# A graph network layer on one core: two small products of a node block move ahead of the node product, and VectorE's share of column copies begins four steps later

## The chip, the core and the metric

The kernel runs on one core of one Trainium2 chip. The metric is the device time of one execution in microseconds (us); a lower time is better. Five engines take part, each with its own instruction stream in a fixed order: TensorE (PE, with its weight loads shown as PEld), VectorE (DVE), ScalarE (ACT), GpSimd (POOL) and SyncE (SP). They wait for each other through semaphores.

## The reference

There are 12,500 nodes with 64 features and 200,000 edges, sorted by their target node. For each edge the reference takes the features of its source and its target, runs them through a two-layer network, does the same with the edge's own 64 features, multiplies the two results and a cutoff factor that depends on the edge's distance, and adds the product to the target node. The sums then go through one more two-layer network per node, and the result is normalised.

```python
nodes = node_state[edges].reshape(num_edges, -1)
gates = ssp(edge_state @ We1 + be1) @ We2 + be2
soft_cutoff = 1.0 - jax.nn.sigmoid(5.0 * (edges_distance - (CUTOFF - 1.5)))
h = ssp(nodes @ Wn1 + bn1) @ Wn2 + bn2
messages = h * (gates * soft_cutoff)
message_sum = jnp.zeros_like(node_state).at[edges[:, 1]].add(messages)
new_state = node_state + (ssp(message_sum @ Ws1 + bs1) @ Ws2 + bs2)
x = _layernorm(x + new_state)          # ssp(v) = softplus(v) - log 2
```

## The kernel before

**Steps.** The edges are cut into 391 steps of 512, each of four lanes of 128 edges (`K = 4`). One loop (variable `i`, from -1) runs all of them in a software pipeline that is written out by hand: the order in which the source issues instructions is the order on each engine. In iteration `i` the first layer of step `i + 1` and the second layer of step `i` are worked on.

**One iteration on TensorE**, in this order: the two biases (`layer1_bias` L299, `layer2_bias` L342); the scatter product of step `i - 2` (`scatter`, L371), whose result is added to the running sums; four transposes of the gathered source features of step `i + 1` (`transposes`, L286, into a tile named tx, of which there are two buffers); the edge product (`layer1_edge`, L304); in most iterations from 91 on the *unread product* (`busy_before_node`, L337), which multiplies constants into a place of the tile z that the next product overwrites and that nothing reads before; the node product (`layer1_node`, L311), which has to wait for ScalarE's copy xT of the transposes; and the second layer (`layer2`, L349 and L354). Up to iteration 90 a table of node products is still being made, one piece for each iteration (`chunk`, L641), in the place where the unread product stands later.

**ScalarE** copies the transposes (xT, L294), makes its column copies, and then the exponential and the logarithm for step `i + 1` (L325, L328). **VectorE** adds the scatter product of the iteration to the sums (`window`, L391), forms the message (`hcut` L363, `message` L367), the softplus of step `i + 1` (L333), the one-hot matrix of step `i + 3` (L280) and its own column copies. The exponential (L325) and `window` read the same tile z, and `window` comes after the exponential.

**Gathers.** POOL fetches the source features of a lane with one indirect DMA (L204), four for each step. The tile xg that they land in has eight buffers, so POOL runs ahead: while TensorE is in iteration `i`, the gathers of step `i + 6` are waiting for the buffer of step `i - 2`, that is for the scatter product of iteration `i`.

**Columns.** For some lanes there is no gather. The features of all nodes also lie transposed in SBUF (xh), and an engine copies the 128 columns of such a lane one by one (L262), 16 in each iteration: ScalarE for lane 2, VectorE for lane 1. Such a lane takes eight iterations, after which VectorE picks the valid half of each column (`choose`, two instructions L274 for each half, so two for each lane), and the node product gets a second part (L314). Which steps have such a lane is worked out by `slots_by_columns`: ScalarE's are taken first, and VectorE's must not be next to one of them. With `COLUMNS_FROM = 8` for both engines, ScalarE's steps are 18, 26, 34, ..., VectorE's 20, 28, 36, ..., 47 of each, and both engines finish a lane in the same iteration (15, 23, 31, ...). The function `four` tells whether a step has four gathers; where step `i + 5` has only three, the unread product of iteration `i` is left out.

**Node blocks.** The nodes are cut into 25 blocks. When the sums of a block are complete, its last network runs in ten parts that are spread over the following iterations by `BLOCK_STEPS`: two of them have TensorE products (`hidden`, L410, which reads the sums; and `layer2` of the block, L438 and L441, which reads a tile that VectorE makes in `ssp`, L433), the others run on ScalarE, VectorE and SP. `hidden` stands two iterations after the block is complete, the block's `layer2` six. In the iteration where one of the two products is due, it is issued after `layer2(i)` of the edges, and its counterpart on VectorE after the softplus. 24 of the blocks have both products inside the loop; the last one comes behind it.

Of the kernel before, what the change touches and what calls it, by code (L numbers as in the profile page):

```python
# [25 lines left out]
P = 128  # L26
# [8 lines left out]
AHEAD = 3  # L35
# [5 lines left out]
BEHIND = 5  # L41
# [3 lines left out]
BLOCK_STEPS = ((2, 3, 4, 4, 6, 7, 8, 9, 10, 14), (2, 3, 3, 4, 5, 6, 7, 8, 9, 10), (1, 2, 1, 2, 3))  # L45
COLUMNS = (16, 16)
BASES = 4
COLUMNS_FROM = 8
XH_PARTS = 4
CUTOFF = 5.0  # L50
EPS = 1e-5
# [4 lines left out]
def node_blocks(N):  # L56

    first = N % NB
    assert N > NB and first % 2 == 0 and first <= HE
    sizes = ([first] if first else []) + [NB] * (N // NB)  # L60
    return [(sum(sizes[:i]), n) for i, n in enumerate(sizes)]


def block_steps(N, NG):

    steps = []
    for at, n in node_blocks(N):
        share = sqrt(min(1.0, (at + n) / N))
        spread = sqrt(share * (1.0 - share) / (NG * GE))
        steps.append(ceil(NG * (share + SPREADS * spread)))  # L70
    return steps


def slots_by_columns(NG):

    slots, taken = [], set()
    for queue in (1, 0):
        columns, n = COLUMNS[queue], 0
        for g in range(NG - 2):
            if (g - 3 - COLUMNS_FROM + 1) * columns >= (n + 1) * P and not {g - 1, g, g + 1} & taken:  # L80
                slots.append((queue, g, queue + 1))
                taken.add(g)
                n += 1
    return sorted(slots)
# [20 lines left out]
def gnn_resnorm_kernel(ctx: ExitStack, tc: tile.TileContext, a: dict, out: bass.AP, E: int):  # L105
# [30 lines left out]
    def tx_tile():  # L136
        return psum.tile([P, NB], F32, name="tx")
# [54 lines left out]
    def padding(g, k):  # L192
        return g * GE + k % 2 * HE + k // 2 * P >= E
# [15 lines left out]
    def four(g):  # L209
        return g < NG and not any(padding(g, k) or (g, k) in by_columns for k in range(K))  # L210
# [21 lines left out]
    own = [[slot for slot in slots if slot[0] == queue] for queue in range(2)]  # L232
    column_tiles, side_tiles, chosen_columns = {}, {}, {}
    column_at, columns_done, whole = [[], []], [0, 0], []

    def columns_left(i, queue):
        return len(own[queue]) * P - columns_done[queue] if i >= COLUMNS_FROM else 0

    def read_columns(i, queue):

# [38 lines left out]
    def onehot(g):  # L279
        last = nc.vector.tensor_tensor(xgs[g][:, :, D:DW], iota, rel[:, g, :].to_broadcast([P, K, W]), OP.is_equal)  # L280
        note(("onehot", g), last)
# [75 lines left out]
    def layer2(g):  # L357
        layer2_edge(g)
        layer2_node(g)
# [121 lines left out]
    with tc.manual_schedule():  # L481
# [64 lines left out]
        def lowest(first, last):  # L546
            part = low[:, first:last]
            nc.vector.tensor_reduce(part, dst_h[:, first:last], AX.X, OP.min)
            nc.vector.tensor_scalar(part, part, 0.0, None, OP.max)
            nc.vector.tensor_tensor(part, part, most[:, first:last], OP.min)  # L550
            n = last - first
            nc.vector.tensor_tensor(spread[:, first:last],
                                    ident.rearrange("p (r q) -> p r q", r=1).to_broadcast([P, n, P]),
                                    part.to_broadcast([P, n, P]), OP.mult)
# [22 lines left out]
        for i, w in enumerate((we2[:D, 0, :], wn2)):  # L577
            n = w.shape[0]
# [83 lines left out]
        with tc.tile_pool(name="finish", bufs=1) as finish:  # L662
            blocks = list(zip(node_blocks(N), block_steps(N, NG)))
            last = NG - 1
            parts, begun, complete, rest = {}, None, 0, []

            def at(f, g, *more):
                if 0 <= g < NG:
                    f(g, *more)

            def behind_by(i):
                close = last - CLOSE
                return [g for g in ([i - 2] if i <= close else []) + ([i - 1] if i >= close else []) if g >= 0]

            for g in range(LOADS - 1):
                load(g)
            for g in range(2):
                onehot(g)
            lowest(1, NR)
            everywhere(1, NR)  # L680
            clear(0, CHUNKS)
            highest()
            for i in range(-1, last - 1):
                now = parts.pop(i, [])
                early = [part for part in now if part.tensor]
                at(load, i + LOADS)
                if i >= 0:
                    at(gather, i + AHEAD, range(K), [("transposes", i)] if i < BEHIND else ())
                layer1_bias(i + 1)
                at(layer2_bias, i)  # L690
                for n, g in enumerate(behind_by(i)):
                    scatter(g, zs[i + 1][:, 1, HE + 2 * n * W : HE + 2 * (n + 1) * W])
                transposes(i + 1, ("load", i + 1), ("gather", i + 1), ("onehot", i + 1))
                xcopy(i + 1)
                columns(i, 1, finish)
                layer1_edge(i + 1)
                c = chunk_of(i, NCH)
                if c is None and four(i + AHEAD + BEHIND - 3):
                    busy_before_node(i + 1)
                if c is not None:  # L700
                    beside_sums = zs[i + 1][:, 1, HE + 2 * W : HE + 2 * W + P]
                    chunk(c, beside_sums)
                layer1_node(i + 1)
                exps(i + 1)
                logs(i + 1)
                if c is not None:
                    keep_chunk(c, beside_sums)
                read_columns(i + 1, 1)
                for g in behind_by(i):
                    window(g)  # L710
                if c is not None:
                    clear(c, c + 1)
                at(layer2, i)
                for part in early:
                    part.tensor(tx_tile())
                at(hcut, i)
                at(message, i)
                softplus(i + 1)
                for part in early:
                    part.others()  # L720
                at(onehot, i + 3)
                read_columns(i, 0)
                columns(i, 0, finish)
                choose(finish)
                for part in now:
                    if not part.tensor:
                        part.others()
                for action in beside.get(i, []):
                    action()
                complete = i  # L730
                if blocks and complete >= blocks[0][1] - PREPARE and not begun:
                    begun = node_block(*blocks[0][0], finish)
                    begun.pop(0).others()
                if blocks and complete >= blocks[0][1]:
                    steps = next(steps for steps in BLOCK_STEPS if i + steps[-1] < last - 1)
                    for n, part in zip(steps, begun):
                        parts.setdefault(i + n, []).append(part)
                    rest = begun[len(steps) :]
                    blocks.pop(0)
                    begun = None  # L740
            assert len(blocks) == 1 and begun and not parts


            begun.pop(2).others()
            transposes(last, ("load", last), ("gather", last), ("onehot", last))
            xcopy(last)
            layer1_bias(last)
            layer2_bias(last - 1)
            scatter(last - 2, zs[last][:, 1, HE : HE + 2 * W])
            layer1_edge(last)  # L750
            layer1_node(last)
            for some in (edge, node):
                exps(last, some)
                logs(last, some)
            square, variance, root, scale, store = (part.others for part in rest)
            square()
            window(last - 2)
            for g in range(last - 1, last + 1):
                if g not in window_at:
                    window_bases(g)  # L760
            layer2(last - 1)
            layer2_bias(last)
            softplus(last, edge)
            layer2_edge(last)
            softplus(last, node)
            layer2_node(last)
            hcut(last - 1)
            message(last - 1)
            scatter(last - 1, tx_tile()[:, : 2 * W])
            variance()  # L770
            root()
            hcut(last)
            message(last)
            scatter(last, tx_tile()[:, : 2 * W])
            window(last - 1)
            window(last)
            hidden, clamp = begun.pop(0)
            hidden(gh_tile())
            scale()
            clamp()  # L780
            store()
            for part in begun:
                node_part(part)
# [5 lines left out]
    with tc.If(far > 0), tc.tile_pool(name="outside", bufs=1) as o:  # L789
# [7 lines left out]
        with tc.For_i(0, NG, 1) as g:  # L797
# [51 lines left out]
            for b in range(NBL):  # L849
# [5 lines left out]
                part = sums[:D, b * NB : (b + 1) * NB]  # L855
# [90 lines left out]
```

## Time and profile before

| what | value |
|---|---|
| median of 3 runs | 2354.7 us (2352.55 to 2364.48) |
| the profiled execution's own time | 2351.35 us |
| its span in the profile | 2349.3 us |
| mean granted TensorE clock | 0.964 |
| busy: PE, DVE, ACT, POOL | 85%, 65%, 64%, 59% of the span |

The profile is of one execution. In its rows, a line such as "L311 PE MATMUL z<-xT,wns" means the instruction of source line 311 on TensorE that writes the tile z from xT and wns; "x4" is a count, since a product of 32-bit numbers is shown as two matmuls for each one in the source; a name in square brackets is the idle time of the engine just before, and what ended it. PEclk is the granted share of the TensorE clock. A view by windows gives, for each stretch from A to B in us, its length and then the busy time of the engines with their number of instructions, the clock, the share of the DMA engines and GB/s.

### The profile page before, as it was taken

The numbers are of one execution on the slowest core, as the hardware profiler recorded it, in microseconds if no ns is written. First come the engines' busy times: TensorE is split into PE (matmuls) and PEld (weight loads), VectorE is DVE, ScalarE is ACT, GpSimd is POOL, SyncE is SP. The second block draws the span as 40 slices with busy tenths as digits, with TensorE's granted clock in tenths as the row PEclk, the third lists the DMA queues.
The fourth block names the chain that finished last, engine by engine and source line by source line (L and its number), as shares of the span: only waits on it lengthen the run. The fifth ranks groups of instructions, "written<-read, shape, count | busy, mean of one in ns | idle before, by whom it ended". The sixth has DMA issues, their size and how long they took to land.

```text
span 2349.3 us, 49245 instructions
## 1 busy us (share of the span) xinstructions
PE 1986.8 (85%) x12011; PEld 1549.9 (66%) x12011; DVE 1536.7 (65%) x9110; ACT 1511.8 (64%) x7412; POOL 1391.5 (59%) x1473
## 2 busy tenths in 40 slices
PE   6788888888888888888888888888888888888877
PEld 4676666666666666666666666666666666666665
DVE  4467666666666666666666667666666676667655
ACT  3466667666666666666667667666666666666653
POOL 6556666566666566666656566665666665556550
PEclk8799999999999999999999999999999999999988
DMA  6332232322222222222222222222222222222220
GB/s 190 95 83 71 64 70 57 79 62 74 60 59 57 54 62 54 59 56 61 55 58 63 52 61 63 59 59 58 59 59 59 59 61 60 55 56 59 60 51 13
DMA packets 162385, 149.51 MB, mean 64 GB/s; under 512 B 40564, under 2 KB 112021, under 8 KB 161962
## 3 DMA queue, kind: packets, MB, share of 16 engines
q1 hardware_dynamic: 114650, 96.55, 15.1%
q0 software_dynamic: 47008, 48.23, 10.9%
q8 instruction: 101, 1.65, 0.3%
q14 instruction: 192, 1.57, 0.2%
q10 hardware_dynamic: 434, 1.50, 0.2%
HBM read 136.50 MB, written 9.62 MB: 62 GB/s over the span
## 4 chain that ended last, share of the span: by engine, by line
PE 76%; issue 12%; DVE 6%; ACT 2%; DVEq 2%; another core or an unknown queue 1%; DMA 1%; POOL 0%; ACTq 0%; POOLq 0%
PE z L311 17%; PE gh L354 13%; PE z L371 10%; PE tx L286 9%; PE gh L349 8%; PE z L304 6%; PE z L337 4%; PE gh L342 3%; PE z L299 3%; DVE column L262 2%; DVEq L245 2%; ACT xT L294 1%; PE tx L410 1%; PE z L314 1%
## 5 line engine op out<-in xcount | busy, mean ns | idle before, releaser
L204 POOL DMA_INDIRECT xg<-in_x,src_i x1469 | 1391.3, 947 | 905.6 <-PE tx L286 378.3
L294 ACT COPY xT<-tx 106x512 f32<-106x512 f32 x391 | 228.6, 585 | 736.1 <-PE tx L286 704.6
L311 PE MATMUL z<-xT,wns 106*128 106x256 f32 x1564 | 464.1, 416 | 270.5 <-issue 238.0
L262 ACT COPY column<-xh 128x4 uint8 x6016 | 608.8, 193 | 0.0
L311 PEld LDWEIGHTS z<-xT,wns 106*128 106x128 f32 x1564 | 273.8, 197 | 420.4 <-issue 336.4
L262 DVE COPY column<-xh 128x4 uint8 x6016 | 486.4, 199 | 11.9 <-issue 6.9
L363 DVE TENSOR_TENSOR h<-gh,cut 128x256 f32<-128x256 f32 x391 | 166.0, 425 | 380.3 <-PE tx L286 260.8
L354 PE MATMUL gh<-consts,s 128*128 128x64 f32 x3128 | 400.2, 272 | 0.0
L354 PEld LDWEIGHTS gh<-consts,s 128*128 128x128 f32 x3128 | 389.6, 196 | 0.1
L328 ACT ACTIVATE u<-u,one 128x768 f32<-128x768 f32 x392 | 365.8, 933 | 13.5 <-ACT u L325 0.8
L333 DVE SCALAR_TENSOR_TENSOR s<-u,z 128x768 f32<-128x768 f32 x392 | 369.3, 942 | 0.4 <-issue 0.3
L391 DVE TENSOR_TENSOR sums<-sums,z 64x42 f32 x778 | 149.4, 192 | 325.5 <-issue 243.1
L325 ACT ACTIVATE u<-z 128x768 f32<-128x768 f32 x392 | 314.7, 803 | 47.2 <-PE z L311 25.5
L371 PEld LDWEIGHTS z<-xg,msg 128*128 128x128 f32 x1556 | 208.9, 195 | 140.9 <-issue 123.4
L371 PE MATMUL z<-xg,msg 128*128 128x84 f32 x1556 | 269.9, 297 | 13.6 <-DVE msg L367 13.5
L349 PEld LDWEIGHTS gh<-consts,s 128*128 128x128 f32 x1564 | 218.8, 196 | 92.7 <-DVE s L333 68.3
L349 PE MATMUL gh<-consts,s 128*128 128x128 f32 x1564 | 269.8, 296 | 11.8 <-issue 7.2
L286 PE MATMUL tx<-consts,xg 128*106 128x128 f32 x1564 | 243.9, 280 | 0.0
L304 PE MATMUL z<-eT,consts 128*128 128x256 f32 x782 | 243.7, 395 | 0.0
L286 PEld LDWEIGHTS tx<-consts,xg 128*106 128x106 f32 x1564 | 187.1, 145 | 1.2 <-issue 1.2
L367 DVE TENSOR_TENSOR msg<-gh,h 128x256 f32<-128x256 f32 x391 | 165.9, 424 | 13.4
L342 PE MATMUL gh<-row,ones 3*128 3x512 bf16 x391 | 149.3, 382 | 0.0
(107 smaller groups left out, 1193.4 us busy)
## 6 DMA issues: line engine op xcount, KB each, us to landing
eT<-in_eT SPq DMA_DIRECT2D x195, 256.0 KB
xg<-in_x,src_i POOLq DMA_INDIRECT x1469
wns<-table SPq DMA_DIRECT2D x782, 21.0 KB
table<-tb SPq DMA_DIRECT2D x14, 448.0 KB
side<-in_sides SPq DMA_DIRECT2D x94, 64.0 KB
y<-in_x SPq DMA_DIRECT2D x24, 128.0 KB
out<-y SPq DMA_DIRECT2D x24, 128.0 KB
xh<-in_xh SPq DMA_DIRECT2D x2, 781.5 KB
```

What stands on the lines that cost most here:

```text
L204: behind(note(("gather", g), nc.gpsimd.indirect_dma_start(out=xg[:, k, :D], out_offset=None, in_=x, in_offset=bass.IndirectOffsetOnAxis(ap ...
L262: copy(column_tiles[slot].bitcast(U8)[:, 4 * r : 4 * r + 4], xh[:, bass.ds(column_at[queue][j] - xh_at, 4)])
L286: ins = nc.tensor.transpose(tx[:, k, :], xgs[g][:, k, :DW], ident)
L294: note(("xcopy", g), nc.scalar.copy(xT, xTs[g]))
L304: nc.tensor.matmul(zs[g][:, 0, :HE], we1.rearrange("a h d -> a (h d)"), eTs[g], start=False, stop=True, skip_group_check=True)
L311: nc.tensor.matmul(zn, wns[:, g % REST, h, :], xTs[g][:, h], start=True, stop=not chosen, skip_group_check=True)
L325: nc.scalar.activation(us[g][:, part], z_of(g)[:, part], AF.Exp)
L328: nc.scalar.activation(us[g][:, part], us[g][:, part], AF.Ln, bias=one)
L333: nc.vector.scalar_tensor_tensor(ss[g].rearrange("p i t e -> p (i t e)")[:, part], us[g][:, part], BIG, z_of(g)[:, part], OP.min, OP.max)
L349: nc.tensor.matmul(v[:, 0, t], ss[g][:, 0, t, :], we2, start=False, stop=False, skip_group_check=True)
L354: nc.tensor.matmul(ghs[g][:, 1, 2 * t + h, :], ss[g][:, 1 + h, t, :], wn2, start=False, stop=h == 1 and t == 1, skip_group_check=True)
L371: ins = nc.tensor.matmul(sc, msgs[g][:, 2 * t : 2 * t + 2, :].rearrange("p h f -> p (h f)"), xgs[g][:, 2 * t : 2 * t + 2, D:DW], start=t = ...
```

## The change

It has two parts. The two TensorE products of a node block (`hidden` and the block's `layer2`) are issued in front of the node product of the same iteration instead of behind the second layer, and in those iterations the unread product is left out. Their counterparts on the other engines stay where they were. And `COLUMNS_FROM` becomes a pair, 12 for VectorE and 8 for ScalarE: VectorE's column copies begin in iteration 12, so its lanes are those of steps 22, 30, 38, ..., in the middle between ScalarE's 18, 26, 34, ...; it has 46 of them instead of 47, and finishes them in iterations 19, 27, 35, ....

```diff
-COLUMNS_FROM = 8
+COLUMNS_FROM = (12, 8)
...
-            if (g - 3 - COLUMNS_FROM + 1) * columns >= (n + 1) * P and not {g - 1, g, g + 1} & taken:
+            if (g - 3 - COLUMNS_FROM[queue] + 1) * columns >= (n + 1) * P and not {g - 1, g, g + 1} & taken:
...
     def columns_left(i, queue):
-        return len(own[queue]) * P - columns_done[queue] if i >= COLUMNS_FROM else 0
+        return len(own[queue]) * P - columns_done[queue] if i >= COLUMNS_FROM[queue] else 0
...
                 c = chunk_of(i, NCH)
-                if c is None and four(i + AHEAD + BEHIND - 3):
+                for part in early:
+                    part.tensor(tx_tile())
+                if c is None and not early and four(i + AHEAD + BEHIND - 3):
                     busy_before_node(i + 1)
...
                 at(layer2, i)
-                for part in early:
-                    part.tensor(tx_tile())
                 at(hcut, i)
                 at(message, i)
```

TensorE, in an iteration with a block's first product (L410, `hidden`; L311 is the node product, L354 the end of the edges' second layer). Before:

```order
L304 MATMUL z<-eT,consts 128x256
L311 MATMUL z<-xT,wns 128x256 x2
L349 MATMUL gh<-consts,s 128x128 x2
L354 MATMUL gh<-consts,s 128x64 x4
L410 MATMUL tx<-sums,consts 128x256 x2
L299 LDWEIGHTS be_82
L299 MATMUL z<-ones_81,be_82 128x256
```

and with the change:

```order
L304 MATMUL z<-eT,consts 128x256
L410 MATMUL tx<-sums,consts 128x256 x2
L311 MATMUL z<-xT,wns 128x256 x2
L349 MATMUL gh<-consts,s 128x128 x2
L354 MATMUL gh<-consts,s 128x64 x4
L299 LDWEIGHTS be_82
L299 MATMUL z<-ones_81,be_82 128x256
```

L410 went from behind L354 to between the edge product and the node product, where the unread product L337 stands in other iterations. The block's second product moved in the same way:

```order
L304 MATMUL z<-eT,consts 128x256
L438 LDWEIGHTS ones_81
L438 MATMUL tx<-rs_84,ones_81 128x256
L441 MATMUL tx<-consts,l_s 128x2x64 x2
L311 MATMUL z<-xT,wns 128x256 x2
L349 MATMUL gh<-consts,s 128x128 x2
L354 MATMUL gh<-consts,s 128x64 x4
```

In all, the unread product is issued 191 times instead of 221. VectorE, at the end of iteration 55 (L262 are the column copies, L274 the choice of the valid half, L391 the next `window`). Before:

```order
L262 COPY column_7053<-xh 128x4 x16
L274 SCALAR_TENSOR_TENSOR chosen_8156<-side_6944,column_6943 64x128 x2
L274 SCALAR_TENSOR_TENSOR chosen_8159<-side_7054,column_7053 64x128 x2
L391 ISA
L391 TENSOR_TENSOR sums<-sums,z 64x42
```

and with the change:

```order
L262 COPY column_7468<-xh 128x4 x16
L274 SCALAR_TENSOR_TENSOR chosen_7960<-side_6745,column_6744 64x128 x2
L391 ISA
L391 TENSOR_TENSOR sums<-sums,z 64x42
```

The four choices that stood together in every eighth iteration are now two and two, four iterations apart.

## The prediction

> **What bounds the kernel now.** I read the page first, then one stretch of the timeline in the middle, then windows from one copy xT to the next. The page alone points to TensorE, which is busy for 85% of the span. Two of its groups speak against that:
>
> ```profile
> span 2349.3 us, 49245 instructions
> L204 POOL DMA_INDIRECT xg<-in_x,src_i x1469 | 1391.3, 947 | 905.6 <-PE tx L286 378.3
> L294 ACT COPY xT<-tx 106x512 f32<-106x512 f32 x391 | 228.6, 585 | 736.1 <-PE tx L286 704.6
> ```
>
> ScalarE waits 704.6 us for the transposes, 1.8 us in each step, and POOL waits for them too. The timeline shows a step with the unread product L337 and then one without:
>
> ```profile
> 1366.12 0.94 POOL L204 DMA_INDIRECT xg<-in_x,src_i  x1 [0.30 <-issue]
> 1366.34 0.60 PE L286 MATMUL tx<-consts,xg 128*106 128x128 f32 x4
> 1367.21 0.59 PE L337 MATMUL z<-consts 128*128 128x256 f32 x2
> 1368.29 0.58 ACT L294 COPY xT<-tx 106x512 f32<-106x512 f32 x1 [1.57 <-PE tx L286]
> 1368.47 0.94 POOL L204 DMA_INDIRECT xg<-in_x,src_i  x1 [1.41 <-PE tx L286]
> 1368.93 1.13 PE L311 MATMUL z<-xT,wns 106*128 106x256 f32 x4 [1.13 <-issue]
> 1370.30 0.80 ACT L325 ACTIVATE u<-z 128x768 f32<-128x768 f32 x1
> 1370.96 0.94 POOL L204 DMA_INDIRECT xg<-in_x,src_i  x1 [0.30 <-issue]
> 1371.22 0.40 DVE L391 TENSOR_TENSOR sums<-sums,z 64x42 f32 x2
> 1372.37 0.60 PE L286 MATMUL tx<-consts,xg 128*106 128x128 f32 x4
> 1373.01 0.59 ACT L294 COPY xT<-tx 106x512 f32<-106x512 f32 x1 [0.94 <-PE tx L286]
> ```
>
> In the first step the transposes end at 1366.94 (1366.34 + 0.60), but xT starts 1.35 us later; in the second it starts 0.04 us after their end (1372.97). What both have in common is POOL: xT starts 2.17 us after the start of the last gather before it (1368.29 - 1366.12), and 2.05 us in the second (1373.01 - 1370.96). POOL in turn starts its next group 0.18 us after xT, because it waits for the same iteration's scatter product. That is a closed loop: release, four gathers at 1.24 us, a tail of some 2.1 us, release. Three gaps of 1.24 plus 2.17 plus 0.18 make 6.07 us; with three gathers it is one gap less, 4.7 to 4.8. Windows from xT to xT on POOL say the same, in the middle of the run (first two rows) and early, where there is no unread product (the next two; the last row is L337 alone):
>
> ```profile
> 707.92:713.97 6.05, 3.79 (x4) 1.00 0.13 29
> 720.04:724.76 4.72, 2.83 (x3) 1.00 0.16 35
> 530.46:536.46 6.00, 3.78 (x4) 1.00 0.27 68
> 536.46:541.29 4.83, 2.83 (x3) 1.00 0.51 129
> 30.00:565.00 535.00, 0.00 (x0) 0.00 (x0) 0.93 0.31 77
> ```
>
> So **an interval lasts 6.05 us with four gathers and 4.72 with three**, with or without the unread product. Why a release should wait for the gathers' tail no row tells; I take the regularity. TensorE's own path from xT to the end of the next transposes is 4.68 us (1368.29 to 1372.97), so it has 1.37 us to spare in a four-gather interval and almost none in a three-gather one. What can be gained lies where an interval is longer than its gathers make it.
>
> **The two products.** Take three intervals from each iteration that has `hidden` (22 iterations, from 55 to 370; 378 and 385 stand in the disturbed end), and the same for the block's `layer2`. Three of the 22 rows, their sum, the sum of the ten whose PEclk is under 1.00, and the sum for `layer2`:
>
> ```profile
> 780.93:801.66 20.73, 11.31 (x12) 0.84 0.23 52
> 1037.59:1054.41 16.82, 10.37 (x11) 1.00 0.26 62
> 2043.54:2065.99 22.45, 11.32 (x12) 0.85 0.20 48
> sum 411.36, POOL 235.88; mean POOL 10.72
> sum 203.68, POOL 110.97; mean POOL 11.10
> sum 380.39, POOL 234.38; mean POOL 10.65
> ```
>
> Of the 66 intervals with `hidden`, 15 have three gathers (those of iterations i where i + 6 has a column lane), so gathers alone ask for 51 x 6.05 + 15 x 4.72 = 379.4 us. They took 411.4: **32.0 us too much**. It is uneven: nothing at 1037.59 (two fours and a three are 16.82), 4.3 at 2043.54. For `layer2`, 16 of 66 have three: 378.0 asked, 380.4 taken, 2.4 us too much. The reason stands in the row of L410:
>
> ```profile
> L410 PE MATMUL tx<-sums,consts 128*128 128x256 f32 x94 | 28.2, 425 | 26.6 <-DVE sums L391 21.9 <-issue 4.4
>   DVE sums L391: 22.5, 15
> L441 PE MATMUL tx<-consts,l_s 128*128 128x128 f32 x92 | 17.0, 307 | 0.0
> L438 PE MATMUL tx<-rs,ones 3*128 3x256 bf16 x23 | 6.4, 278 | 0.0
> ```
>
> `hidden` reads the sums, so at its old place it waits for the `window` of its own iteration, and that one comes after the exponential (L391 at 1371.22, behind L325, which ends at 1371.10) and after whatever VectorE had queued. The worst case:
>
> ```profile
> 2043.36 0.20 DVE L391 TENSOR_TENSOR sums<-sums,z 64x42 f32 x1 [0.88 <-issue]
> 2047.96 0.59 DVE L274 SCALAR_TENSOR_TENSOR chosen<-side,column 64x128 f32<-64x128 int32 x2 [0.43 <-issue]
> 2049.38 0.41 DVE L391 TENSOR_TENSOR sums<-sums,z 64x42 f32 x2 [0.83 <-issue]
> 2049.93 2.05 PE L410 MATMUL tx<-sums,consts 128*128 128x256 f32 x4 [2.98 <-DVE sums L391]
> ```
>
> TensorE stood for 2.98 us until `window` came at 2049.38, behind four choices, and then L410 took 2.05 us because the clock had fallen. In front of the node product it needs only the `window` of the iteration before, which had ended at 2043.56, 5.8 us before the one it waited for. So the wait goes.
>
> What the product costs at the new place: 28.2 us in 23.5 blocks is 1.20 us for L410, and 17.0 + 6.4 us in 23 blocks is 1.02 for L438 and L441. The room in front of the node product, where the release was late, is the idle 1.13 of the L311 row plus what L337 held back, at least 0.4 (1367.21 to the end at 1367.80, less what ran under L304): 1.5, enough. Behind a three-gather interval the release was not late and the node product starts up to 1.2 us later; the interval then has four gathers, and 1.37 to spare. If that cover were gone, each product would cost its 1.0 to 1.2 us. Behind L311 the exponential, L349 and L391 queue; L391 has to wait until L410 has read, but L410 precedes L311 and so the exponential. I put down 3 us for places where the previous `window` (as at 2043.56, 0.02 after xT) or `ssp` is itself late, and 0.4 for `layer2`. Together: -32.0 + 3 = -29, bounds -32 and -17 (half of what lies in the ten windows stays, below); and -2.4 + 0.4 = -2.
>
> In the ten windows with PEclk under 1.00 lie 203.7 - (27 x 6.05 + 3 x 4.72) = 26.2 of the 32.0 us. [...] The trace has the clock down after 1.76 us of idle time (below), so I go by the trace.
>
> **The columns.** VectorE's lanes move to the middle between ScalarE's. One lane fewer is one gather more: 6.05 - 4.72 = +1.3 us. The four choices now come two and two. Choices and a block's `scale` are what makes VectorE late. A case of each kind, the first of `scale` alone in a three-gather interval with its window and the next, the second of four choices and `scale`:
>
> ```profile
> 1195.96 0.16 DVE L465 SCALAR_TENSOR_TENSOR scaled<-scaled,rstd 128x4 f32<-128x4 f32 x1 [1.14 <-DVE scaled L464]
> 1199.77 1.22 PE L349 MATMUL gh<-consts,s 128*128 128x128 f32 x4 [1.76 <-issue]
> 1196.23:1205.31 9.08, 4.40 (x5) 0.68 0.24 63
> 1205.31:1210.59 5.28, 3.16 (x4) 0.90 0.17 36
> 838.12 0.58 DVE L274 SCALAR_TENSOR_TENSOR chosen<-side,column 64x128 f32<-64x128 int32 x2
> 838.98 0.58 DVE L274 SCALAR_TENSOR_TENSOR chosen<-side,column 64x128 f32<-64x128 int32 x2 [0.29 <-DVE chosen L274]
> 840.72 0.40 DVE L391 TENSOR_TENSOR sums<-sums,z 64x42 f32 x2
> ```
>
> The first cost 9.08 + 5.28 - 2 x 6.05 = 2.3 us, since the softplus was late, TensorE stood and the clock fell to 0.68. That `scale` now falls into a four-gather interval, which takes 2.3 us away. But all choices now lie in three-gather intervals (iterations 0 and 4 modulo 8), and in seven of them there is also a `scale`. In the second case four choices cost 1.44 us (838.12 to 839.56) and the release at 841.1 was still met; with two, VectorE is done 0.7 us sooner, in an interval that is 1.3 us shorter: late by 0.6, which TensorE's next, long interval covers. I expect one of the seven to cost 2.3: net 0, bounds -2.3 and +14. The unread product that is gone from 30 iterations counts at nothing, since the gathers set the pace.
>
> **Sum.** -29 - 2 + 1.3 + 0 = -30 against the profiled execution's 2351.35 us (its span and 2.05 around it). It lies 3.4 us under the median shown; the forecast on the median's scale is 2354.7 - 30 = **2324 us**, with its own range 2313 to 2333.
>
> **Rivals.** *The clock falls for another reason* than the wait, and half of the 26 us in the ten windows stays: 2324 + 13 = 2337. For it: windows with a wait hardly longer than others have the clock down too, and even by a tenth only. Against it: where nothing waits (1037.59) it is 1.00. [...] *The stall only moves*: VectorE is late anyway in those places, and L349 waits for the softplus instead of L410 for `window`. For it: at 2049.38 VectorE had everything behind the choices. Against it: POOL's next release was not due before 2043.54 + 6.05 = 2049.59. Then only some 5 us are left: 2350. *VectorE becomes the bound in the short intervals*, the slower side: choices, with gaps like the 1.14 at 1195.96, stand in 93 three-gather intervals at 2.3 us each where they make the softplus late. From 13 on they eat the gain, from 19 on the kernel is slower by more than 0.5%; a quarter of them, 23, makes 2324 + 53 = 2377. For it: the case at 1196. Against it: the one at 838. *The unread product sets the pace*, and 30 iterations lose 1.33 us more: 2284; the early windows without L337 speak against it.
>
> **How the numbers follow.** Forecast 0.64, other reason for the clock 0.16, moved stall 0.10, VectorE's bound 0.07, unread product 0.03. The measurement tells a difference of about 0.5%, 12 us, from none. Faster: 0.64 + 0.16 + 0.03 = 0.83; same 0.10, slower 0.07. The range reaches from a gain of 47, the bounds of all terms with something for the end of the run, to most of the third case: 2308 to 2346; outside are the last two rivals and a part of the third.
>
> **What would show it.** L410 idle for `sums` falls from 22.5 us to under 6. The 22 stretches of three intervals come to some 14 to 30 us less than 411, and nearly all have PEclk 1.00; the mean clock rises over 0.97. Ordinary intervals stay at 6.05 and 4.72, L204 counts 1470. If intervals of three gathers grow to over 5.2, or L349 waits much longer for the softplus than before, VectorE's case is there. If four-gather intervals without the unread product shrink, the pace was read wrongly.

## The result, and the profile after

The changed kernel takes 2341.51 us (median of six runs, 2332.26 to 2349.53), the kernel before beside it 2355.87 us (2352.55 to 2364.48): a ratio of 0.9939, 95% interval 0.992 to 0.9957. It is faster, by 14 us instead of the 30 forecast. The profiled execution is the slowest of the six (2349.53 us, only 1.8 us less than the one profiled before), so its trace shows the losses larger than the median has them.

The page of the change, then the groups of L410 and of L349 (busy time, mean ns, then the idle time before and what ended it):

```profile
span 2347.7 us, 48985 instructions
L204 POOL DMA_INDIRECT xg<-in_x,src_i x1470 | 1391.9, 947 | 904.7 <-PE tx L286 370.3
```

```profile
L410 PE MATMUL tx<-sums,consts 128*128 128x256 f32 x94 | 25.3, 392 | 2.8 <-DVE sums L391 2.8
L349 PE MATMUL gh<-consts,s 128*128 128x128 f32 x1564 | 278.8, 303 | 8.8 <-issue 4.5 <-DVE s L333 2.9
```

L410 no longer waits: its idle time fell from 26.6 to 2.8 us, and its mean from 425 to 392 ns, close to its median of 379, the time at a clock of 1.00 (634 at 0.50). L349 does not wait longer for the softplus than before (2.9 us, 3.5 then; the weight loads of this line wait 76.4 us for it and waited 68.3; loads run beside other products, PE being busy for 1977.6 and PEld for 1543.6 of 2347.7 us). The 22 stretches of three intervals from each `hidden`, as in the prediction; an ordinary row between the two long ones, and the sum:

```profile
1336.93:1359.64 22.71, 10.98 (x12) 0.81 0.16 37
1421.23:1438.03 16.80, 10.44 (x11) 1.00 0.22 51
1992.14:2015.97 23.83, 11.23 (x12) 0.80 0.19 46
sum 391.09, POOL 236.36; mean POOL 10.74
```

391.1 us instead of 411.4. Their gathers ask for 378.0 (now 16 of the 66 intervals have three), and the two rows with a clock of 0.8 hold nearly all of the 13.1 us left: 22.71 and 23.83 where two fours and a three make 16.82. The other twenty are where their gathers put them, with the clock at 1.00.

So most of the forecast gain is there, and something else was lost. Three stretches of the whole run show where: iterations 1 to 38 and 38 to 91 (in both the table is being made and there is no unread product), and 91 to 376. The columns are the length, TensorE's busy time and the granted clock; first the kernel before, then the change:

```profile
37.80:269.84 232.04, 192.45 (x1123) 0.89 0.33 82
269.84:576.40 306.56, 263.13 (x1623) 0.97 0.28 66
576.40:2238.68 1662.28, 1430.22 (x8737) 0.98 0.25 59
```

```profile
38.50:283.74 245.24, 204.26 (x1123) 0.84 0.32 79
283.74:597.51 313.77, 269.09 (x1623) 0.94 0.27 64
597.51:2240.08 1642.57, 1408.81 (x8679) 0.99 0.26 60
```

From iteration 91 on the change is 19.7 us faster, although one interval more has four gathers. Before it, it is 13.2 and 7.2 us slower, with the same number of three-gather intervals (7 and 13) and a lower clock. In the early part `hidden` and the block's `layer2` occur only once (iterations 55 and 59), so what differs in the program there is the columns. Not all of the 13.2 us can be put down to them, though: a run with the old columns, below, takes 241.14 us for the first stretch, 9.1 more than the kernel before with the same instructions.

One early three-gather interval (iteration 44) and the one behind it, from xT to xT, with POOL's busy time in the second place and the clock in the third; then the clock in four stretches of 3.41 us, here with TensorE's busy time in the second place:

```profile
319.69:325.91 6.22, 3.03 (x4) 0.73 0.12 23
325.91:331.55 5.64, 3.58 (x4) 1.00 0.33 80
```

```profile
296.46:299.87 3.41, 3.39 (x12) 0.50 0.09 19
316.94:320.35 3.41, 2.01 (x15) 1.00 0.35 105
320.35:323.77 3.42, 3.42 (x12) 0.50 0.16 32
344.25:347.66 3.41, 3.41 (x12) 0.50 0.10 19
```

6.22 us where three gathers ask for 4.72, of which the next interval gives back 0.4. The clock goes with it: it is 0.50 for exactly one such stretch, and the row before it has TensorE busy for 2.01 of 3.41 us. TensorE's timeline shows the idle time in that row, in front of the node product, and then how slow the two layers run:

```profile
318.55 0.39 PE L641 MATMUL z<-consts,sums 65*128 65x128 f32 x2
320.33 2.08 PE L311 MATMUL z<-xT,wns 106*128 106x256 f32 x4 [1.40 <-issue]
322.20 1.06 PE L349 MATMUL gh<-consts,s 128*128 128x128 f32 x4
323.05 1.35 PE L354 MATMUL gh<-consts,s 128*128 128x64 f32 x8
```

The node product took 2.08 us (1.13 in the middle of the run before), and L349, L354 behind it are slow too (1.06 and 1.35 us, where there they took 0.71 and 1.00). A four-gather interval has 1.37 us to spare for this, a three-gather one 0.04 (4.72 less 4.68). And the stretches at half clock begin 23.9 us apart (296.46, 320.35, 344.25): the shortest records of the granted clock in this trace last 3.413 us, and 7 x 3.413 = 23.89. This much is read from one trace, the experiments come below: with a three-gather interval in every fourth place, four intervals are 3 x 6.05 + 4.72 = 22.87 us, and with the 1.1 us of such a loss some 24.0, so the next fall meets the same kind of interval again. In the records of the granted clock of the change, nine falls begin between iterations 38 and 91, eight of them in three-gather intervals (40, 44, 48, 52, 64, 68, 72, 76). In the kernel before there are five (40, 49, 65, 74, 89), all in four-gather intervals. The later runs without more unread products bear this out in part: a second run of the change has seven falls there, all in three-gather intervals, two runs with the old columns have four and six, all in four-gather intervals; but of the runs with the change's columns below, the columns alone have three of five falls in three-gather intervals, the change with two spare gathers three of six, and the change without any unread product none of four. So the meeting of falls and short intervals is common with these columns, but no rule. In a four-gather interval a short fall can cost nothing, as these two intervals of the kernel before show (iteration 40, which holds such a stretch, and 41; together 12.10 = 2 x 6.05):

```profile
280.61:286.82 6.21, 3.85 (x5) 0.73 0.11 21
286.82:292.71 5.89, 3.77 (x4) 1.00 0.26 63
```

The two long rows with `hidden` are another matter. POOL around the first of them:

```profile
1339.60 0.94 POOL L204 DMA_INDIRECT xg<-in_x,src_i  x1 [0.30 <-issue]
1343.25 0.94 POOL L204 DMA_INDIRECT xg<-in_x,src_i  x1 [2.72 <-issue]
...
1346.99 0.94 POOL L204 DMA_INDIRECT xg<-in_x,src_i  x1 [0.30 <-issue]
1348.43 0.94 POOL L204 DMA_INDIRECT xg<-in_x,src_i  x1 [0.49 <-issue]
...
1352.17 0.94 POOL L204 DMA_INDIRECT xg<-in_x,src_i  x1 [0.30 <-issue]
```

```profile
1346.02 0.60 PE L286 MATMUL tx<-consts,xg 128*106 128x128 f32 x4
1352.39 1.22 PE L311 MATMUL z<-xT,wns 106*128 106x256 f32 x2 [4.91 <-issue]
```

POOL starts the first gather of a step 2.72 us after the last one of the step before, where some 1.3 is usual (1.36 in front of the gather at 1337.11), and waits for nothing that the profile shows. From then on eight gathers follow one another without a pause. The transposes end at 1346.62, but xT (1351.76) and the node product (1352.39) are held until near the end of that series. The clock is 0.50 in the interval behind it (1351.76 to 1359.64). Counted from zero at the program's first gather, this one has the number 855. Such pauses of 2.7 to 2.9 us stand in front of number 113, 537, 855 and 1279, always 106 or a multiple of it apart. The numbers between them (219, 325, ...) are not the first of their step, and the idle time in front of them is 0.3 to 0.6 us. In the kernel before, only 855 and 1279 are the first of a step (3.73 and 2.85 us).

### The profile page after: what moved, and what is told of

Read it like the earlier page. It is cut to its first block, busy times and chain, and to the rows that moved or that the text cites. A ratio compares the mean times of both kernels' runs of the same rounds, so it can differ in the third digit from the quotient of the medians.

```text
span 2347.7 us, 48985 instructions
## 1 busy us (share of the span) xinstructions
PE 1977.6 (84%) x11949; PEld 1543.6 (66%) x11949; DVE 1529.0 (65%) x8979; ACT 1513.7 (64%) x7412; POOL 1392.2 (59%) x1474
## 4 chain that ended last, share of the span: by engine, by line
PE 79%; issue 12%; DVE 4%; ACT 2%; DVEq 1%; another core or an unknown queue 1%; DMA 0%; ACTq 0%
PE z L311 18%; PE gh L354 14%; PE z L371 10%; PE gh L349 9%; PE tx L286 9%; PE z L304 6%; PE gh L342 3%; PE z L299 3%; PE z L337 3%; DVEq L245 1%; DVE column L262 1%; PE tx L410 1%; ACT xT L294 1%; PE z L314 1%
## 5 line engine op out<-in xcount | busy, mean ns | idle before, releaser
L204 POOL DMA_INDIRECT xg<-in_x,src_i x1470 | 1391.9, 947 | 904.7 <-PE tx L286 370.3
L311 PE MATMUL z<-xT,wns 106*128 106x256 f32 x1564 | 469.8, 420 | 309.9 <-issue 269.4
L262 ACT COPY column<-xh 128x4 uint8 x6016 | 608.8, 193 | 0.0
L311 PEld LDWEIGHTS z<-xT,wns 106*128 106x128 f32 x1564 | 276.5, 198 | 454.1 <-issue 372.1
L262 DVE COPY column<-xh 128x4 uint8 x5888 | 479.3, 199 | 11.2 <-issue 6.8
L354 PE MATMUL gh<-consts,s 128*128 128x64 f32 x3128 | 405.7, 274 | 0.0
L354 PEld LDWEIGHTS gh<-consts,s 128*128 128x128 f32 x3128 | 396.0, 198 | 0.1
L391 DVE TENSOR_TENSOR sums<-sums,z 64x42 f32 x778 | 151.0, 194 | 358.5 <-issue 237.9
L349 PEld LDWEIGHTS gh<-consts,s 128*128 128x128 f32 x1564 | 221.7, 199 | 99.4 <-DVE s L333 76.4
L349 PE MATMUL gh<-consts,s 128*128 128x128 f32 x1564 | 278.8, 303 | 8.8 <-issue 4.5
L367 DVE TENSOR_TENSOR msg<-gh,h 128x256 f32<-128x256 f32 x391 | 166.0, 424 | 13.4
```

The costliest lines, as they stand in the source:

```text
L204: behind(note(("gather", g), nc.gpsimd.indirect_dma_start(out=xg[:, k, :D], out_offset=None, in_=x, in_offset=bass.IndirectOffsetOnAxis(ap ...
L262: copy(column_tiles[slot].bitcast(U8)[:, 4 * r : 4 * r + 4], xh[:, bass.ds(column_at[queue][j] - xh_at, 4)])
L311: nc.tensor.matmul(zn, wns[:, g % REST, h, :], xTs[g][:, h], start=True, stop=not chosen, skip_group_check=True)
L349: nc.tensor.matmul(v[:, 0, t], ss[g][:, 0, t, :], we2, start=False, stop=False, skip_group_check=True)
L354: nc.tensor.matmul(ghs[g][:, 1, 2 * t + h, :], ss[g][:, 1 + h, t, :], wn2, start=False, stop=h == 1 and t == 1, skip_group_check=True)
```

## The experiments

There are two questions: whether the products bring the 30 us and the columns take half of it back, and, if so, whether they do it by the clock in the early iterations, by POOL's pauses, or by VectorE. The runs came on three chips, on which the kernel before took 2356.5 us (the first four), 2390.3 (the next four) and 2391.9 us (the last four). Only ratios, or runs of one chip, are compared. The change itself was not repeated beside the first four; its 2341.51 us are those of the result, where the kernel before took 2355.87. All edits are made to the changed kernel.

**One part alone.** The products only:

```diff
-COLUMNS_FROM = (12, 8)
+COLUMNS_FROM = (8, 8)
```

> Only the two products are moved; the columns are as before (VectorE's lanes at steps 20, 28, ...). Theory A (the gain of the products is whole, and the columns give half of it back: POOL stops at every 106th gather, which costs 3 to 8 us where that gather is the first of its step, in two places here and four in the change; and early on the four-step rhythm of the new columns lets the clock fall): 2318 to 2330, POOL's long idle times before a step's first gather only at gathers 855 and 1279 (iterations 221 and 334), early intervals as in the kernel before. Rival B (the products themselves bring only some 14 us, and the columns nothing): 2338 to 2344.

Measured: 2328.15 us, ratio 0.9885 (0.9858 to 0.9912). The products bring 28 us; rival B falls. POOL's pauses are at 855 and 1279 (2.70 and 2.81 us), and those at 113 and 537 are gone. Its three stretches:

```profile
38.42:279.56 241.14, 201.10 (x1123) 0.85 0.32 80
279.56:587.74 308.18, 263.37 (x1623) 0.96 0.27 66
587.74:2224.39 1636.65, 1398.40 (x8677) 0.99 0.25 60
```

The last is 25.6 us shorter than in the kernel before; against the change the three are 4.1, 5.6 and 5.9 us shorter. The columns only, with the products back behind the second layer:

```diff
-                for part in early:
-                    part.tensor(tx_tile())
-                if c is None and not early and four(i + AHEAD + BEHIND - 3):
+                if c is None and four(i + AHEAD + BEHIND - 3):
...
                 at(layer2, i)
+                for part in early:
+                    part.tensor(tx_tile())
```

> Only the columns are moved; the products stand behind the second layer as before. Theory A: slower than before, 2362 to 2378: 7 us in iterations 38 to 90, 5 to 13 us in two more stops of POOL (iterations 23 and 136), 1.3 us for the added gather. Rival B: within 3 us of the kernel before, 2352 to 2358.

Measured: 2367.9 us, ratio 1.0039 (1.0013 to 1.0066). By itself the second part of the change makes the kernel slower, by 9 to 11 us, in the lower half of what was expected; rival B falls. The two parts add up: 0.9885 x 1.0039 = 0.9924, against 0.9939 for both. The profiled execution, the slowest of the twelve (2384.13 us), doesn't have its loss in the early part alone: against the kernel before, its stretches are 10.3, 6.0 and 19.0 us longer.

**The early clock against VectorE.** The unread product is issued up to iteration 90 too. The choices, the lanes and the number of gathers stay as they are in the change:

```diff
-                if c is None and not early and four(i + AHEAD + BEHIND - 3):
+                if not early and four(i + AHEAD + BEHIND - 3):
```

> The change, and the unread product also in the iterations up to 90, beside the table's product. Theory A (the idle 1.35 us before the node product lets the clock fall in the early three-gather intervals): those intervals go from 6.2 to 4.7 us, no clock of 0.5 between iterations 38 and 90, the time 6 to 9 us below the change's, about 2334. Rival V (the choices make VectorE late there): the intervals stay at 6.2 us, the time 0 to 4 us above the change's.

Measured: 2324.68 us, ratio 0.9869 (0.9843 to 0.9896), 17 us below the change and more than expected. Its stretches, then iterations 44 and 45:

```profile
38.09:270.39 232.30, 196.85 (x1183) 0.93 0.34 82
270.39:573.99 303.60, 269.71 (x1698) 1.00 0.27 67
573.99:2211.50 1637.51, 1406.57 (x8679) 0.99 0.26 60
```

```profile
305.35:310.05 4.70, 2.83 (x3) 1.00 0.14 29
310.05:316.12 6.07, 3.78 (x4) 1.00 0.30 73
```

Iteration 44 takes 4.70 us instead of 6.22, with the same choice in front of it. Between iterations 38 and 91 the clock is 1.00 throughout, and 303.60 us is what the gathers ask for (40 x 6.05 + 13 x 4.72 = 303.4). VectorE's work is unchanged, so rival V falls for these intervals. The stretch from 1 to 38 is 12.9 us shorter too, which was not in the sum; how much of it is the filling is open, since this stretch took 232.0 to 245.2 us in the runs of this chip without filling.

**POOL's pauses.** Two gathers more ahead of all others shift the count by two and leave the rest of the program:

```diff
+        spare = prep.tile([P, D], F32, name="spare")
+        for _ in range(2):
+            nc.gpsimd.indirect_dma_start(
+                out=spare, out_offset=None, in_=x,
+                in_offset=bass.IndirectOffsetOnAxis(ap=src_i[:, 0, :1], axis=0))
         for g in range(AHEAD):
             gather(g)
```

> The change, and two gathers more ahead of all others, into a place that nothing reads; nothing else is touched. Theory A (POOL stops at every 106th gather, counted from the program's start): the stops in front of a step's first gather leave iterations 23, 136, 221 and 334 and come at 79, 192 and 277; three instead of four, so 0 to 8 us below the change's time. Rival R (these stalls belong to the data or the code of those steps): they stay where they are. Rival N (they are chance): they come anywhere. Under R and N the time is that of the change or up to 2.5 us more.

Measured: 2337.81 us, ratio 0.9927 (0.9904 to 0.9951), 3.7 us below the change, which is within the noise. The pauses are at numbers 325, 749 and 1067, as expected:

```profile
518.34 0.99 POOL L204 DMA_INDIRECT xg<-in_x,src_i  x1 [2.86 <-issue]
```

```profile
1171.51 1.00 POOL L204 DMA_INDIRECT xg<-in_x,src_i  x1 [2.79 <-issue]
```

```profile
1657.12 0.95 POOL L204 DMA_INDIRECT xg<-in_x,src_i  x1 [2.68 <-issue]
```

Iterations 79 and 80, and after them the old places 136, 221 and 334:

```profile
516.83:526.17 9.34, 6.00 (x7) 0.94 0.23 56
526.17:534.06 7.89, 1.44 (x2) 0.50 0.05 10
850.43:855.12 4.69, 2.83 (x3) 1.00 0.15 34
1335.69:1341.73 6.04, 3.78 (x4) 1.00 0.30 75
1982.93:1988.97 6.04, 3.79 (x4) 1.00 0.24 41
```

So the pause follows the count of gathers and not the step, its data or its code, and rivals R and N fall: the old places are as short as any other. One pause can cost 6.5 us (9.34 + 7.89 for a four and a three, 10.77). The whole kernel gained little, but the two gathers have a price of their own: xT of iteration 1 starts at 44.94 us instead of 38.50. So this run doesn't tell what the pauses cost in the whole.

**No unread product at all** in the change:

```diff
-                if c is None and not early and four(i + AHEAD + BEHIND - 3):
-                    busy_before_node(i + 1)
```

> The change without any unread product (a product whose result nothing reads, so no output is touched). Theory A: the idle time before the node product grows to 1.3 us and more everywhere, the clock falls as it does up to iteration 90, three-gather intervals go from 4.69 to about 6.2 us wherever the idle time lies within one stretch of the clock's steps: 2370 to 2430. Rival P (the unread product only takes time of TensorE, or sets the pace of the four-gather intervals): 2284 to 2341.

Measured: 2442.86 us, ratio 1.0226 (1.0202 to 1.025), thus 2.9% or 67 us more than the change by the ratios, some 2409 us on the scale of the first chip and inside the expected 2370 to 2430; the mean clock is 0.887. The loss lies behind iteration 90: from 91 to 376 it takes 1723.20 us at a clock of 0.88, where the change's second run, below, takes 1662.75 at 0.99. Four intervals, the second of them with three gathers:

```profile
740.54:747.23 6.69, 4.16 (x5) 0.66 0.29 68
747.23:752.61 5.38, 2.66 (x4) 0.78 0.13 26
752.61:758.31 5.70, 3.58 (x4) 1.00 0.32 79
758.31:764.44 6.13, 3.78 (x4) 1.00 0.31 61
```

The last, with the clock at 1.00, is no shorter than a four-gather interval with the unread product (6.14 at the median in the next run, on the same chip; 6.15 in the rows of the change's second run, below). So the unread product does not set the pace, and rival P falls; what it does is to hold the clock.

**Old columns with the filling, and spare gathers with them.** On the second chip: the first edit and the third together; then with the two spare gathers; then with `COLUMNS_FROM = (10, 8)` instead of `(8, 8)`, which gives the same lanes but parts the choices two and two.

> The products moved, the columns as before the change, and the unread product also up to iteration 90. Theory A: against the change with that same filling (2324.7 us) two of the four stops of POOL before a first gather are gone (23 and 136), the other two stay: 2314 to 2321. Rival F (the filling alone has given back all that the columns took): 2322 to 2328.

> The kernel of the run before in this list (products moved, old columns, filling) and two spare gathers ahead of all others. Theory A: of the stops before a first gather only one is left, at iteration 277: 2 to 8 us less, of which the two gathers may take back up to 2.5. Rival R: no stop moves, the time is the same or up to 2.5 us more.

> As the run before in this list, but VectorE begins its columns two iterations later than ScalarE: the lanes are the same, the four choices that stand in one iteration are split two and two, both in front of four-gather intervals. Theory A: the choices cost nothing once the clock stays up, so within 2 us of the run before. Rival V (choices make VectorE late): 3 to 8 us less.

Measured: 2356.18 us, ratio 0.9856 (0.9835 to 0.9876); 2369.72 us, 0.9911 (0.9891 to 0.9931); 2365.57 us, 0.9891 (0.9874 to 0.9908). The absolute figures of the first expectation were those of the first chip; its ratio would be 2322.5 us there, which is rival F. The second expectation was wrong in its sign: fewer pauses, and 13.5 us more. Some of it is the two gathers themselves at the start: there the first interval became 5.6 us longer. The rest are single falls of the clock scattered over the run (its mean is 0.984 and then 0.967 in the profiled executions), which no run parts further. From the second run to the third it is 4.2 us less, which is in the range of rival V and not within theory A's 2 us, but the intervals overlap: it stays open whether parting the choices helps.

**Both edits crossed on one chip.** What was still open was how much of the columns' cost is the clock, and how much the pauses (four with the change's columns, two with the old ones). So the change, old columns, filling, and both, side by side:

> The change itself once more, as the measure for the three runs beside it on the same chip: a ratio to the kernel before of 0.992 to 0.996 under every theory.

> The products moved, columns as before, no filling, beside the change on one chip. Theories C (the clock in the early iterations is the larger part of what the columns cost) and S (POOL's stops before a first gather are the larger part) both: 9 to 16 us below the change. Rival B (the two differ by the chip alone): within 4 us.

> The change with the unread product also up to iteration 90, on the same chip. Theory C: 12 to 18 us below the change. Theory S: 5 to 9 us below it, the four stops still cost what they did.

> Products moved, old columns, with the filling, on the same chip. Theory C: the columns are worth little once the clock stays up, so within 5 us of the run with the change's columns and filling, on either side. Theory S: 6 to 12 us below it, because two of four stops are gone.

| | change's columns | old columns |
|---|---|---|
| no filling | 2375.49 us, 0.9922 (0.9898 to 0.9947) | 2363.49 us, 0.9892 (0.9871 to 0.9912) |
| unread product also up to iteration 90 | 2358.31 us, 0.9857 (0.9837 to 0.9877) | 2358.27 us, 0.9858 (0.9839 to 0.9878) |

Without the filling the change's columns cost 12.0 us by the medians (0.0030 by the ratios, 7 us), with it nothing. The filling gives 17.2 us with the change's columns and 5.2 with the old ones. Both are as theory C has them, and theory S misses both: with the filling, two pauses more leave no trace in the median. The runs of one cell lie 7 to 17 us apart, and the intervals of the upper row overlap a little. On the first chip the change and the run with the old columns are apart by more than their intervals, so that the columns cost something is clear of noise; how much is not. The stretch from 38 to 91: the change, then the old columns, both without the filling, and the change with it:

```profile
284.45:605.29 320.84, 275.23 (x1623) 0.93 0.27 63
276.62:589.76 313.14, 271.21 (x1623) 0.94 0.28 65
```

```profile
275.93:584.86 308.93, 270.86 (x1697) 1.00 0.28 65
```

Here, where no pause of POOL lies, the change's columns cost 7.7 us without the filling (5.6 on the first chip). Over what the gathers ask for, the profiled executions without the filling lose 5 to 14 us in this stretch with the change's columns (five runs) and 3 to 6 with the old ones (three); with the filling all six lose under 6. The rest can't be placed by the traces: without the filling the change is also 9.0 us slower before iteration 38 and 8.0 behind 91. Nor do the pauses cost nothing: against the pace of 6.14 and 4.74 us, the five intervals around each come to an estimated 18 us too much in the run with the change's columns and the filling (four pauses), and to 7 in the one with the old columns (two). The latter has falls of the clock in other places instead (iterations 57, 199, 215, 257), for which no run gives the reason.

The lower row of the table is also the fastest version: some 33.6 us under the kernel before on that chip.

## Why the prediction was right or wrong

**The pace was read rightly.** Intervals are still 6.05 and 4.72 us where nothing disturbs them, L204 counts 1470, and without the unread product a four-gather interval is no shorter.

**The products were right in mechanism and size.** The prediction put -29 and -2 for them; alone they brought 28.3 and 28.4 us on two chips (2356.45 to 2328.15, and 2391.9 to 2363.49). L410's wait for the sums went from 21.9 to 2.8 us (from 22.5 to 3.4 where the prediction read its sign), the 22 stretches lost 20.3 us, twenty of them have the clock at 1.00. The rival that the clock falls there for another reason holds for the two other rows alone, where POOL's pauses keep 12.9 us in this execution; in the twenty it came up with the wait gone. The rival that the stall only moves falls: L349 itself waits no longer than it did.

**The columns were the step that failed.** The prediction's sum has them at "net 0, bounds -2.3 and +14", beside +1.3 for the added gather. They cost 13.4 us on the first chip (2341.51 less 2328.15) and on the third 12.0 by the medians and 7 by the ratios, up to the upper bound, and the reason was not the one given. It looked at VectorE: choices and `scale` in three-gather intervals, at 2.3 us each. In iteration 44 of the change the choice stands there and the interval is 1.5 us too long, as that rival would have it, but with the filling the same choice costs nothing. What the prediction left out is that the early iterations have no unread product, so TensorE idles 1.3 to 1.4 us before the node product of a step behind two four-gather intervals, and the clock falls in some of these places (iterations 40, 44, 48 and 52 of the change, with 1.38, 1.40, 1.33 and 1.38 us) and not in others (iteration 80, with 1.41, which took 4.68 us at a clock of 1.00). It had read windows from that part (30 to 565 us) and taken from them only that the pace is the same. The row has PEclk 0.93, and it was not asked what these falls cost and in which intervals they lie. With the filling, which leaves the columns as they are, their cost is gone from the median. The prediction had no term either for POOL's pauses, of which the change's columns make four instead of two.

**"The unread product that is gone from 30 iterations counts at nothing, since the gathers set the pace"** was right in its number for those iterations, where the moved products fill the place, but the reason hid the product's work: taken out everywhere it costs 67 us.

**Of the signs named**, the mean clock (0.963, not over 0.97) and three-gather intervals over 5.2 us told that something was wrong, but the second would have been put down to VectorE. L349's wait was what parted the two, and on TensorE it had not grown.

The forecast's own -30 against 14: of the 16 us that are missing, 2 or 3 are the products' 28.3 instead of 31, and the others are the columns, with 7 to 13 instead of 1.3. That this cost hangs on the clock of the early iterations is shown by the runs with the filling; in the traces 5.6 and 7.7 us of it stand between iterations 38 and 91, and how the rest parts between the clock before iteration 38 and POOL's pauses stays open.

## What to carry to other kernels

A product that nothing reads can be what holds the clock (here the granted clock behind iteration 90 is 0.99 with it and 0.88 without, and 67 us hang on it): before its place is given away, or a rhythm is changed in a part that has none, look at TensorE's busy time and clock in that part by itself. Idle time that cost nothing in an interval with slack cost 1.5 us in one without (iteration 44, 6.22 us for 4.72), so a change of rhythm is to be judged by which intervals the falls of the clock land in, not by the mean. And where two parts of a change go out together, each should be costed in each stage of the run; here the gain of one part hid the loss of the other in the total.

## What the runs showed of the hardware

The clock falls at places of a fixed grid: in the change's records of the granted clock every stretch at 0.50 lasts 3.413 us or a whole multiple of it (6.83, 10.24, 13.65, 20.48), save the one that the trace ends with, and their starts lie whole multiples of it apart (296.46, 320.35, 344.25). At 320.35 it fell after a stretch with TensorE busy for 2.01 of 3.41 us, with an idle time of 1.40. Which stretches lose it and which don't isn't settled: between iterations 1 and 376 of the change, stretches of 3.41 us at full clock kept it with a busy share of 0.57 to 0.66, and others lost it with up to 0.66 and once 0.79, so the busy share alone does not tell it.

In the change POOL pauses some 1.4 us longer (2.7 to 2.9 instead of 1.3) at every 106th gather when that is the first of a step, and with two gathers more the place moves with the count (2.86, 2.79 and 2.68 us at 325, 749 and 1067). What it does there no row tells. Such a late start can grow to 6 or 7 us, as in the rows of 22.71 and 23.83 us, where POOL runs two steps' gathers in one series, xT stands near its end and the clock falls behind it; why the release waits for the series is not shown. Where the clock holds, it costs some 1.3 us (both pauses in the run with the old columns and no filling on the third chip; the interval with number 537 in the change, 7.35 us for 6.05 at a clock of 1.00).

The pace differs from chip to chip: 6.15 us for a four-gather interval of the change on the third chip, where the first chip has 6.05, while three gathers take 4.73:

```profile
720.86:727.01 6.15, 3.79 (x4) 1.00 0.29 72
727.01:731.74 4.73, 2.83 (x3) 1.00 0.17 35
```

With 297 of 391 steps of four gathers in the kernel before, 0.1 us each makes some 30 of the 35 us between the kernel before on the one chip and on the other.
